# New queue places for the last reads and the tile plan, and new order offsets, in a convolution, Mamba and expert kernel

## Chip, cores and metric

The kernel runs on one core of one Trainium2 chip. Times are device microseconds of one execution. A profile is one further execution, recorded by the hardware profiler; its span runs from the first to the last instruction.

## The reference

The input is two images of 256 channels and 48 by 48 pixels (4608 tokens in all). Layer 0 is a hybrid of local attention and convolution. Layer 1 is a Mamba block over the tokens, followed by a mixture of eight experts of which each token uses two. What matters here is layer 1:

```python
t = t + _L1_attn_ref(_ln_t(t), ...)      # Mamba: projection, convolution, scan over the state, output projection
t = t + _L1_ffn_ref(_ln_t(t), ...)       # experts
# in _L1_ffn_ref:
top_w, top_i = jax.lax.top_k(gate_logits, TOP_K)
for e in range(E):
    h = jax.nn.gelu(xf @ W1[e] + b1[e], approximate=False)
    out = out + w_dense[:, e:e + 1] * (h @ W2[e] + b2[e])
```

## The kernel before

Tokens are worked in 36 chunks of 128 tokens; three chunks make a block of 384. After layer 0 come four parts.

**Mamba.** For each chunk the kernel projects (`cv` for the convolved half, `z` for the gates), turns (`tx`), forms the weighted input `xw`, adds to the state (`pst`), reads it (`ps`, `yi`), multiplies within the chunk (`py`), gates the result (`yz`), sums its squares (`sq`, `sm`, `ss`) and projects it back (`out`). TensorE (PE) does `cv`, `z`, `tx`, `pst`, `ps`, `py`, `ss` and `out`; GpSimd (POOL) does `dx`, `xw`, `yb`, `yz`, `sm` and `rg`; the others do the rest. `keep` stores the finished chunk to the table `acc` in DRAM.

**Gates and stores of rows.** The chunks are gated in seven groups, `GROUPS = (6, 6, 6, 6, 6, 4, 2)`. A group computes logits, the two best experts, and a row for each token and expert in the table `xs` (`place`, `row`, `g10`). `u2` writes the normalised token, and `put` (L1678) stores it with an indirect DMA that POOL issues, two for each chunk, 72 in all.

**Early tiles.** One expert, the one with most rows among the first 24 chunks, begins before Mamba ends: three tiles of 256 rows are fetched from `xs` (`efetch`, on SP, the queue of SyncE; there is room for one in SBUF at a time), turned on PE (`et`), copied by ScalarE (`ext`), and run through `eu` (L1804, up), `eg` (L1812, gelu), `ed` (L1820, down). `ea` (L1832, on VectorE) adds the bias, `es` (L1839) scales by `eweight` (L1788), which is reduced from `eown` (L1780, on POOL), and `eput` (L1842) adds the rows to `acc` with an accumulating indirect DMA. There are two places for the outputs of `ea`, so the third tile's waits for the first tile's two `eput`.

**Usual tiles.** `plan` computes on VectorE which expert and which rows every further tile has. SP loads these values, fetches rows (L2024) and weights (L2014, L2016), and 37 tiles follow: `turn`, `up` (L2080), `down` (L2123 or L2108), `finish` (L2089 scale, L2090 accumulating store). The first `turn` is queued on VectorE behind the last early `ea`.

**Results.** The sums in `acc` are read back in twelve blocks (`load_sums`, L2195), turned on PE (L2219), copied by VectorE and ScalarE (L2222) and stored (L2225) by SP and by ScalarE's queue in turn. Blocks 0 to 7 are read while the last usual tiles run. Blocks 8 to 11, the late reads, wait for the last accumulating store.

The order of Mamba, of the gates and of the early tiles is written by a planner, `Flow`. Every operation has an engine, a cost in nanoseconds, needs and buffers; the planner runs through a model of time, and of the operations that are ready on an engine the one with the lowest rank goes first. The rank is the due time of its chunk less the longest tail of work behind it less an offset for its kind:

```python
return {k: o["due"] - tail[k] - self.lead.get(self.kind(k), 0) for k, o in self.ops.items()}, after
```

The offsets are the table `LEAD1`. What the planner traces is the order in which the engines and SP work; only POOL's order is bound more loosely, by `issue_after` (issue order alone). All of `experts` and `results` is outside the planner: a scheduler orders it within its dependencies, with `issue_after` and `keep_in_program_order` where the code says so.

Of the kernel before, what the change touches and what calls it, by code (L numbers as in the profile page):

```python
# [37 lines left out]
P = 128  # L38
# [32 lines left out]
E, HID = 8, 1024  # L71
NHC = HID // P

TR = 256
CAP = B * N
PART = CAP + TR
EARLY, NEARLY = 3, 3
# [151 lines left out]
class Kernel:  # L229
# [688 lines left out]
    def mamba(self, ctx):  # L918

        nc = self.nc
        self.ps = self.pool("ps", 1, space=bass.MemoryType.PSUM)
        self.used_banks = ["zbank0", "zbank1"]

        room = dict(bank=6, zbank=2, cvbank=2, t=3, xn=2, xc=2, bc=3, cz=2, z=2, btt=2, xd=3, xw=2,
                    mt=4, yi=1, y=4, sq=2, state=3, rd=2, u2=2, ex=1, ext=1, ehid=2, ey=2)
        self.begin_flow(self.pool("m", 1, ctx), room, self.PACE1, self.LEAD1)
        zeros = self.pool("cz", 1, ctx)
        self.cz = [zeros.tile([P, 2, TB], F32, name=f"cz{i}") for i in range(room["cz"])]  # L930
        for t in self.cz:
            nc.gpsimd.memset(t, 0.0)
        for k in range(B * NBLK):
            self.norms(k)
            self.project_block(k)
            self.decays_of(k)
            for c in range(k * NJ, (k + 1) * NJ):
                self.chunk(c)
        first = 0
        for g, n in enumerate(GROUPS):  # L940
            self.gate(g, first, n)
            first += n
        self.early_expert(sum(GROUPS[: EARLY + 1]))
        for i in range(NEARLY):
            self.early_tile(i, sum(GROUPS[: EARLY + 1]))
        self.run_flow()

    PACE1 = 16387
    LEAD1 = {
        "al": -287523, "begin": 279332, "btt": 547186, "ct": -286059, "cum": -1917, "cv": 4243,  # L950
        "decayed": 580164, "dg": 31429, "dt": 47275, "dx": -122176, "ea": -540346, "ebegin": 83800,
        "ed": -318255, "efetch": 54828, "eg": -25970, "eown": -201872, "eplan": -259253,
        "eput": -235403, "er": 11828, "es": -860893, "et": -422487, "etoken": -124013,
        "eu": -436657, "ew": 409693, "eweight": -208246, "ex": -43880, "ext": 233628, "from": -4920,
        "g10": -236552, "g5": 182590, "g6": -32896, "g8": 451102, "g9": -229727, "ge": 6967,
        "gm": 76638, "gmrs": 125702, "grs": 147058, "gsm": -98577, "gsw": -443388, "gw": -513534,
        "head": -233622, "kap": 45673, "keep": -259171, "lg": 101202, "mm": 234795, "mo": -242501,
        "mrs": 274104, "msw": -365601, "mt": -42112, "n2": -300607, "nt": 130491, "number": -184813,
        "out": -70294, "pg": -24498, "place": -128574, "ps": 331262, "pst": 114708, "put": -219828,
        "py": 171510, "rd": 184258, "rg": -26951, "row": 47214, "rs": 219345, "rs1": -133005,  # L960
        "s0": 349893, "s4": 378544, "s5": 226237, "scores": -354133, "silu": -107647,
        "silub": 149134, "silux": 61236, "sm": 498786, "spread": -381240, "sq": -108133,
        "sr": -62966, "ss": -24463, "st": -62401, "state": -200685, "stats": -473991, "su": -4356,
        "tap": 199461, "tb": 11998, "tc": 509331, "tx": 705626, "u2": -301346, "xc": 387790,
        "xd": 75748, "xo": 176627, "xt": 78392, "xw": 264171, "ya": 88604, "yb": 4326, "yi": -10587,
        "yz": -93682, "z": -15541,
    }

    def norms(self, k):
# [556 lines left out]
    def gate(self, g, first, n):  # L1526
# [3 lines left out]
        nc, T = self.nc, self.tiles  # L1530
# [118 lines left out]
        def place():  # L1649
# [5 lines left out]
           uses=[("bank", ("count", g))])  # L1655
# [19 lines left out]
        for i, c in enumerate(chunks):  # L1675
            for q in range(2):
                def put(i=i, c=c, q=q):
                    ins = nc.gpsimd.indirect_dma_start(  # L1678
                        self.xs, bass.IndirectOffsetOnAxis(ap=of("rows")[:, i, q : q + 1], axis=0), T["u2", g][:, i, :],
                        None,  # L1680
                    )
                    self.tc.declare_no_dep(ins.ins, group="rows", reason="every row of the table is written once")
                    self.tc.add_to_no_dep_group("rows", ins.ins)
                    if c >= sum(GROUPS[: EARLY + 1]):
                        self.tc.add_to_no_dep_group("late rows", ins.ins)

                op(("put", (c, q)), "POOL", 1020, put, ("g10", g), ("g8", g), ("u2", c), ("number", g), uses=[("u2", g)])


    def flat(self, b):  # L1690
# [55 lines left out]
    def early_tile(self, i, seen):  # L1746
# [82 lines left out]
        def add():  # L1829
            at = 3 + self.flow.slot["ey", i]  # L1830
            y = T["ey", i] = self.x[1][:, :, at * TR : (at + 1) * TR]
            self.last_add = vec.tensor_tensor(y, T["bank", ("ed", i)].rearrange("p (j q) -> p j q", j=2),  # L1832
                              bcast(bt[:, NHC : NHC + C], 1, [P, 2, C]), ALU.add)

        op("ea", "DVE", 690, add, ("ed", (i, NHC // 2 - 1)), *free, takes=[("ey", i)], uses=[("bank", ("ed", i))])
        for j in range(2):
            def scale(j=j):
                y = T["ey", i][:, j, :]
                nc.scalar.activation(y, y, AF.Identity, scale=T["eweight", i][:, j : j + 1])  # L1839

            def put(j=j):
                ins = pool.indirect_dma_start(  # L1842
                    self.acc, bass.IndirectOffsetOnAxis(ap=T["etoken", i][:, j : j + 1], axis=0), T["ey", i][:, j, :],
                    None, compute_op=ALU.add,
                ).ins
                self.tc.declare_no_dep(ins, group="early", reason="a token has one row of an expert")
                self.tc.declare_no_dep(ins, group="late keeps", reason="later chunks have other rows")
                self.tc.add_to_no_dep_group("early", ins)

            op(("es", (i, j)), "ACT", 390, scale, ("ea", i), ("eweight", i))  # L1850
            op(("eput", (i, j)), "POOL", 1500, put, ("es", (i, j)), ("etoken", i), *[("keep", c) for c in range(seen)],
               uses=[("ey", i)])

    def plan(self):

        nc, begun = self.nc, [5 * TR] * NH
        n, k, tid = P, CAP // TR, self.c["tid"]
        tri = self.c["tri"].rearrange("p (a b) -> p a b", a=E)

        def new(*shape, dtype=F32):  # L1860
            size = int(np.prod(shape))
# [15 lines left out]

        last_rows = new(E, dtype=I32)
        vec.tensor_scalar(last_rows, self.taken, 1.0, None, ALU.add)
        rows = new(3, E)  # L1880
        vec.tensor_sub(rows[:, 0, :], self.taken, self.begin)
        vec.tensor_scalar(rows[:, 1, :], rows[:, 0, :], float(-P), None, ALU.add)
# [60 lines left out]
        for which, row, behind in ((pwhich, prow, late), (swhich, srow, None)):  # L1943
# [14 lines left out]
            vec.tensor_scalar(to[:, 0, :], row, float(E * PART), None, ALU.min)  # L1958
            vec.tensor_scalar(to[:, 1, :], which, float(E - 1), float(P), ALU.min, ALU.mult)
            where.append(to)  # L1960
        return last_rows, where, many

    def value(self, ap, engines, most):

# [12 lines left out]
    def experts(self, ctx):  # L1977
# [159 lines left out]
                    finish(i, y, j)  # L2137
            del weights[i], turned[i], hidden[i]

        ends, where, many = self.plan()  # L2140
        for e in range(E):
            fill(e)
        load(0)
# [2 lines left out]
        load(1)  # L2146
        load(2)
        fetch(2)
        with self.tc.issue_after(self.last_add.ins):
            turn(0)  # L2150
            weight_sums(0)

# [38 lines left out]

    def load_sums(self, g, group=None):

        nc = self.nc
        get = (nc.sync, nc.scalar)[g % 2 if group is None else 0].dma_start(  # L2195
            self.sums_block(g), self.acc[g * TB : (g + 1) * TB, :].rearrange("(p j) c -> p j c", j=NJ)
        )
        if group:
            self.tc.add_to_no_dep_group(group, get.ins)

    def results(self, pool):

        nc = self.nc

        first, size, n = BEFORE // NJ, 2 * TB, 0
        for g in range(0, B * NBLK, 2):
            b, blk = divmod(g, NBLK)
            if g == first:
                for i in range(first, B * NBLK):
                    self.load_sums(i)  # L2210
            for k in range(NH):
                if n % (WMAT // size) == 0:
                    space = pool.tile([P, WMAT], F32, tag="wt", name="o")
                o = space[:, n % (WMAT // size) * size :][:, :size].rearrange("p (i t) -> p i t", i=2)
                n += 1
                for i in range(2):
                    ps = self.bank()
                    for j in range(NJ):
                        nc.tensor.transpose(  # L2219
                            ps[:, j * P : (j + 1) * P], self.sums_block(g + i)[:, j, k * P : (k + 1) * P], self.ident  # L2220
                        )
                    (nc.vector.tensor_copy, nc.scalar.copy)[i](  # L2222
                        o[:, i].rearrange("c (p j) -> c j p", j=NJ), ps[:, :TB].rearrange("c (j p) -> c j p", j=NJ)
                    )
                (nc.sync, nc.scalar)[k].dma_start(self.out[b, k * P : (k + 1) * P, blk * TB : (blk + 2) * TB], o)  # L2225
# [133 lines left out]
```

## Time and profile before

| what | value |
|---|---|
| median of 3 runs | 1307.5 us |
| the runs | 1303.49, 1307.5, 1307.64 us |
| the profiled execution | 1306.41 us, span 1304.4 us |
| PE, share of the span busy | 95% |
| PE weight load | 75% |
| VectorE (DVE) | 71% |
| ScalarE (ACT) | 61% |
| POOL | 43% |
| indirect stores L1678 | 72, 72.7 us busy on POOL |

Shares are averages over stages with different limits. A line of who waited for whom gives engine, tile and line, then what ended the wait, then the total in us, how many times, and the longest. A line of the timeline gives start and length in us, engine, line, operation, tiles and shapes, and in brackets the idle time of the engine before it with what ended it. A row of busy time by stretch gives the stretch, its length, the busy us of PE, PE's weight load, DVE, ACT and POOL, then the granted PE clock, the busy share of the DMA engines, and GB/s. PE's matmuls overlap each other, so that their ends are modelled.

### The profile page before, as it was taken

The page shows a single profiled execution, that of the slowest core. Times are in us where ns is not written, and L with a number is a line of the kernel's source. Part 1 is how long each engine was busy: PE and PEld are TensorE (multiplying, and loading weights), DVE is VectorE, ACT ScalarE, POOL GpSimd, SP SyncE. Part 2 cuts the span into 40 slices and gives each one's busy share as a digit, 9 for nine tenths or more (in the row PEclk, how much of TensorE's full clock was granted, in tenths as well). Part 3 has the DMA queues.
Part 4 walks back from the last instruction along what each step waited for, and adds up shares of the span by engine and source line. Part 5 has one row for each costly group of instructions (what it writes and reads, how often), then busy time and mean ns, then how long its engine had stood idle before and what let it go on. Part 6 is the DMA issues. An engine that isn't in the chain of part 4 may idle for free.

```text
span 1304.4 us, 23542 instructions
## 1 busy us (share of the span) xinstructions
PE 1237.6 (95%) x8048; PEld 984.3 (75%) x8048; DVE 929.0 (71%) x2425; ACT 796.3 (61%) x1956; POOL 557.9 (43%) x769
## 2 busy tenths in 40 slices
PE   4999999997899999999999998999999999999995
PEld 3566766665567776767676787999999999999994
DVE  5899999999577878888787654655655565556442
ACT  2598968898899877979696742433343333333342
POOL 4312230210367798879888872222221212221220
PEclk9999999999799999999999998999999999999998
DMA  8331322211132243424446148567667657766756
GB/s 297 109 103 41 117 83 79 74 50 31 65 99 80 85 133 101 139 89 160 137 122 189 54 142 277 156 191 247 184 228 227 212 183 234 234 190 199 231 176 206
DMA packets 101657, 194.10 MB, mean 149 GB/s; under 512 B 10635, under 2 KB 82652, under 8 KB 96604
## 3 DMA queue, kind: packets, MB, share of 16 engines
q1 hardware_dynamic: 84732, 167.72, 38.2%
q0 software_dynamic: 14400, 19.74, 7.9%
q10 hardware_dynamic: 2404, 5.11, 1.1%
q8 instruction: 65, 1.06, 0.3%
q14 instruction: 56, 0.46, 0.1%
HBM read 154.24 MB, written 43.23 MB: 151 GB/s over the span
## 4 chain that ended last, share of the span: by engine, by line
PE 46%; POOL 10%; DVE 3%; issue 3%; ACT 2%; DMA 1%; ACTq 0%; SPq 0%; DVEq 0%; POOLq 0%
PE bank L2080 19%; PE po L2123 15%; POOL xs L1678 4%; PE bank L916 2%; PE bank L1450 1%; PE po L2108 1%; PE bank L902 1%; PE zbank L916 1%; POOL sq L1457 1%; POOL y L1424 1%; POOL y L1442 1%; PE bank L1820 1%; PE bank L1432 1%; PE bank L1804 1%; POOL y L1331 1%
## 5 line engine op out<-in xcount | busy, mean ns | idle before, releaser
L2090 POOL DMA_INDIRECT acc<-ey,token x70 | 109.2, 1560 | 368.0 <-ACT ey L2089 322.9
L2080 PE MATMUL bank<-ext,wt 128*128 128x256 f32 (+1 forms) x1152 | 241.3, 368 | 0.0
L2084 ACT ACTIVATE hid<-bank,bt 128x256 f32<-128x256 f32 (+1 forms) x288 | 132.4, 461 | 170.9 <-PE bank L2080 166.6
L2080 PEld LDWEIGHTS bank<-ext,wt 128*128 128x128 f32 x1152 | 207.0, 190 | 25.0
L681 POOL COPY kp<-kp 128x10 f32<-128x10 f32 (+1 forms) x60 | 24.7, 412 | 179.8 <-DVE kp L674 179.8
L592 DVE SCALAR_TENSOR_TENSOR x<-hid,w2r,x 128x1128 f32<-128x1128 f32 (+3 forms) x72 | 100.1, 1394 | 0.4 <-ACT hid L586 0.2
L2123 PE MATMUL po<-ts,ss 128*128 128x128 f32 x768 | 96.2, 275 | 0.0
L916 PE MATMUL bank<-xn,win 128*128 128x387 f32 x240 | 93.0, 511 | 1.6 <-ACT t L998 1.6
L1128 DVE SCALAR_TENSOR_TENSOR xc<-bank,vec,xc 128x384 f32<-128x384 f32 x144 | 86.7, 612 | 9.2 <-ACT xc L1117 8.6
L2123 PEld LDWEIGHTS po<-ts,ss 128*128 128x128 f32 x768 | 90.9, 192 | 0.0
L1344 ACT ACTIVATE mt<-mt,cum 128x128 f32<-128x128 f32 x288 | 87.9, 394 | 0.0
L800 ACT ACTIVATE prob<-prob,top 128x308 f32<-128x308 f32 x144 | 78.4, 553 | 15.3 <-DVE top L789 15.0
L1678 POOL DMA_INDIRECT xs<-u,rows x72 | 72.7, 1009 | 16.0 <-issue 14.3
L2127 ACT COPY u<-po 128x128 f32<-128x128 f32 x32 | 8.5, 266 | 113.9 <-PE po L2123 113.9
L1450 PE MATMUL bank<-wout,y 128*128 128x264 f32 x288 | 71.3, 392 | 1.2 <-DVE yi L1409 1.2
L2067 DVE TENSOR_TENSOR ss<-hid 128x512 f32<-128x512 f32 x32 | 22.1, 691 | 70.3 <-ACT hid L2084 70.3
L916 PE MATMUL zbank<-xn,win 128*128 128x384 f32 x192 | 71.0, 491 | 0.3 <-ACT z L1246 0.3
L806 ACT ACTIVATE prob<-prob,rden 128x308 f32<-128x308 f32 x144 | 67.8, 552 | 3.7 <-DVE rden L855 3.7
L582 DVE SCALAR_TENSOR_TENSOR hid<-xp,vec,hid 128x1175 f32<-128x1175 f32 (+1 forms) x48 | 68.5, 1428 | 0.1
L2123 PE MATMUL po<-wt,hid 128*128 128x128 f32 x496 | 65.5, 275 | 0.0
L789 DVE CUSTOM_DVE_ANT_0 prob<-banks,cst 128x308 f32<-128x308 f32 x144 | 61.7, 473 | 4.9 <-PE banks L779 4.6
L916 PEld LDWEIGHTS bank<-xn,win 128*128 128x128 f32 x240 | 43.2, 196 | 23.9 <-issue 3.7
(335 smaller groups left out, 3004.2 us busy)
## 6 DMA issues: line engine op xcount, KB each, us to landing
wt<-in_We SPq DMA_DIRECT2D x36, 2048.0 KB
mt<-decays SPq DMA_DIRECT2D x36, 512.0 KB
ex<-xs SPq DMA_DIRECT2D x36, 265.0 KB
rd<-decays SPq DMA_DIRECT2D x68, 128.0 KB
val<-vtab SPq DMA_DIRECT2D x72, 110.0 KB
bt<-in_We SPq DMA_DIRECT2D x36, 136.0 KB
vraster<-vout SPq DMA_DIRECT2D x18, 256.0 KB
acc<-x SPq DMA_DIRECT2D x36, 128.0 KB
```

Of the source, the lines that this page charges most:

```text
L582: nc.vector.scalar_tensor_tensor(dst, src, w[:, k : k + 1], dst, ALU.mult, ALU.add)
L592: nc.vector.scalar_tensor_tensor(dst, src, w[:, k : k + 1], dst, ALU.mult, ALU.add)
L800: nc.scalar.activation(t, t, AF.Exp, bias=T["top", c][:, a : a + 1], scale=-1.0, accum_out=T["den", c][:, a : a + 1])
L916: self.nc.tensor.matmul(ps, lhsT=lhs(k), rhs=rhs(k), start=k == 0, stop=k == NH - 1)
L1128: nc.vector.scalar_tensor_tensor(out(), T["bank", ("cv", at)][:, i : i + TB], wc[:, i : i + 1], out(), ALU.mult, ALU.add)
L1344: nc.scalar.activation(t, t, AF.Relu, bias=at_s, scale=-1.0)
L1450: nc.tensor.matmul(ps[:, : C + E], lhsT=T["y", c][:, m, :], rhs=self.l1["wout"][:, m, :], start=m == 0, stop=m == NZ - 1,)
L1678: ins = nc.gpsimd.indirect_dma_start(self.xs, bass.IndirectOffsetOnAxis(ap=of("rows")[:, i, q : q + 1], axis=0), T["u2", g][:, i, :], None,)
L2080: nc.tensor.matmul(ps[:, :rows], lhsT=w1[:, k, c * P : (c + 1) * P], rhs=xt[:, k, :], start=k == 0, stop=k == NH - 1,)
L2084: nc.scalar.activation(hid[:, c, :], ps[:, :rows], AF.Gelu, bias=bt[:, c : c + 1])
L2090: put = nc.gpsimd.indirect_dma_start(self.acc, bass.IndirectOffsetOnAxis(ap=token[:, j : j + 1], axis=0), y, None, compute_op=ALU.add)
L2123: nc.tensor.matmul(p[name], lhsT=v[a][:, c], rhs=v[w][:, c], start=c == 0, stop=c == NHC // 2 - 1)
```

## The change

It has four parts.

1. All late reads go to SP, one after another in program order, which is behind the four early stores of SP in `results`. Before, two of the four were on ScalarE's queue, and both pairs stood ahead of the stores.
2. `plan` is split: the first part computes the ends of the experts' rows, and `plan_tiles` the rest. `plan_tiles` is queued on VectorE behind the second early tile's `ea`. The adds are kept in a table, `self.adds`, in place of `self.last_add`.
3. The planner counts 1315 ns for a `put` in place of 1020, and 1980 for an `eput` in place of 1500.
4. The table `LEAD1` has a new offset for each of its 95 kinds.

```diff
+        self.adds = {}
         self.early_expert(sum(GROUPS[: EARLY + 1]))
...
     LEAD1 = {
-        "al": -287523, "begin": 279332, "btt": 547186, "ct": -286059, "cum": -1917, "cv": 4243,
...
+        "al": -290978, "begin": 28518, "btt": 903929, "ct": -258969, "cum": 138318, "cv": 4160,
...
-                op(("put", (c, q)), "POOL", 1020, put, ("g10", g), ("g8", g), ("u2", c), ("number", g), uses=[("u2", g)])
+                op(("put", (c, q)), "POOL", 1315, put, ("g10", g), ("g8", g), ("u2", c), ("number", g), uses=[("u2", g)])
...
-            self.last_add = vec.tensor_tensor(y, T["bank", ("ed", i)].rearrange("p (j q) -> p j q", j=2),
+            self.adds[i] = vec.tensor_tensor(y, T["bank", ("ed", i)].rearrange("p (j q) -> p j q", j=2),
...
-            op(("eput", (i, j)), "POOL", 1500, put, ("es", (i, j)), ("etoken", i), *[("keep", c) for c in range(seen)],
+            op(("eput", (i, j)), "POOL", 1980, put, ("es", (i, j)), ("etoken", i), *[("keep", c) for c in range(seen)],
...
         last_rows = new(E, dtype=I32)
         vec.tensor_scalar(last_rows, self.taken, 1.0, None, ALU.add)
+        return last_rows, partial(self.plan_tiles, new, piece)
+
+    def plan_tiles(self, new, piece):
...
-        ends, where, many = self.plan()
+        ends, plan_tiles = self.plan()
+        with self.tc.issue_after(self.adds[NEARLY - 2].ins):
+            where, many = plan_tiles()
...
-        with self.tc.issue_after(self.last_add.ins):
+        with self.tc.issue_after(self.adds[NEARLY - 1].ins):
             turn(0)
             weight_sums(0)
...
-        get = (nc.sync, nc.scalar)[g % 2 if group is None else 0].dma_start(
+        get = self.nc.sync.dma_start(
...
-                    self.load_sums(i)
+                    self.tc.keep_in_program_order(self.load_sums(i))
```

## Prediction

> **What bounds the kernel now.** I read the slices of the page first, then the busy time by stretch, then who waited for whom in Mamba, in the early tiles and at the end. The slices show four stages: layer 0 to about 322 us, Mamba to about 752 (the last output projection), the rest of the early tiles to 800, 37 usual expert tiles to 1280, and the results.
>
> ```profile
> PE   4999999997899999999999998999999999999995
> ...
> POOL 4312230210367798879888872222221212221220
> ...
> 350.00:745.00 395.00, 381.47 (x2419) 274.73 (x2418) 320.49 (x908) 325.83 (x765) 325.17 (x440) 0.99 0.40 119
> 815.00:1247.00 432.00, 432.00 (x2922) 404.22 (x2921) 250.53 (x644) 155.30 (x365) 99.88 (x64) 1.00 0.67 210
> ```
>
> The columns after the length are busy PE, weight load, DVE, ACT, POOL. In the expert stage PE never stops (432.00 of 432.00), and nothing the change touches is in it: no gain there. In Mamba PE works 381 of 395 us, and POOL 325, to which the pauses around its 72 indirect stores come. Waits, PE in 440 to 745, then POOL in 440 to 783:
>
> ```profile
> PE bank L1460 <- POOL sq L1457: 6.0, 6, 2.1
> PE bank L1370 <- POOL xw L1316: 2.5, 2, 2.1
> PE bank L1432 <- DVE mt L1352: 1.2, 2, 1.0
> ...
> POOL xs L1678 <- issue: 14.3, 65, 0.3
> ```
>
> So what PE loses in Mamba it loses mostly to POOL (8.5 us), and POOL's stores (L1678) cost 0.3 us each beyond their own 0.99: a store follows a store after 1.28 us (770.48, 771.76, 773.13 in the timeline), where the plan counted 1020 ns. The early tiles:
>
> ```profile
> DVE eweight L1788 <- POOL eown L1780: 8.9, 1, 8.9
> ...
> PE bank L1820 <- ACT x L1812: 5.2, 1, 5.2
> ...
> 782.18 0.17 DVE L1788 TENSOR_REDUCE eweight<-eown 128x2 f32<-128x16 f32 x1 [8.93 <-POOL eown L1780]
> ...
> 786.75 0.68 DVE L1832 TENSOR_TENSOR x<-bank,wt 128x512 f32<-128x512 f32 x1
> ...
> 788.79 3.06 PEld L1820 LDWEIGHTS bank<-wt,x 128*128 128x128 f32 x8 [5.59 <-ACT x L1812]
> 788.79 3.78 PE L1820 MATMUL bank<-wt,x 128*128 128x256 f32 x8 [5.18 <-ACT x L1812]
> ```
>
> Read upwards: PE stands for 5.2 us, for a gelu on ACT; ACT stood at the scale behind the add L1832; the add stood on DVE behind the plan (782.3 to 786.7) and this behind eweight, which waited 8.9 us for eown on POOL, queued behind the last stores. After the stall eight matmuls take 3.78 us instead of 1.89. The first usual tile starts at 800.23. The end:
>
> ```profile
> ACT o L2222 <- DMA acc<-ey,token: 4.9, 1, 4.9
> ...
> 1282.00:1284.00 2.00, 0.02 (x1) 0.00 (x0) 0.72 (x2) 0.00 (x0) 0.00 (x0) 1.00 0.59 66
> ...
> 1292.00:1294.00 2.00, 1.99 (x16) 1.54 (x16) 0.86 (x2) 1.21 (x2) 0.00 (x0) 1.00 1.03 416
> ```
>
> ACT holds two of the four late reads, which wait for the last scatter (landed at 1283.7), and its copies for the early output stand behind them for 4.9 us; from 1286 to 1302 the DMA engines are full (381 GB/s mean).
>
> [...]clock 0.54 from 788.8 to 795.2 behind the 5.2 us stall. [...]1283 ns a load; the trace has 1.28 us. The order has 33 loads instead of 35, but ACT is not at its limit, so I count nothing.
>
> **The change part by part.** The sum is made against the profiled execution, 1306.4 us (span 1304.4). [...]
>
> *New offsets and costs of the stores.* No instruction is added; the five engines' orders change in Mamba. I read both orders and made running totals of measured durations: POOL from its groups (yz 1.274, yb 1.276, dx 1.044, xw 1.040, a pair of sq sums 1.19, rg 0.564, a store 1.28), PE from the chain (out 1.78 a chunk, py 1.02, ps 1.09, a cv or z block 1.3, an up or down step 1.75, the rest from its groups). Totals hardly differ: POOL's last store ends after 395.5 us of work before and 395.9 after; PE has 445.3 in both. What differs is how they mesh. POOL runs behind PE by a lag. For POOL not to wait, the lag must be at least PE's total ahead of py (or tx) less POOL's ahead of yz (xw) of that chunk; for PE not to wait, at most PE's total ahead of out, ss or pst less POOL's ahead of yz, sq or xw. From chunk 8 on, the room between the highest lag asked so far and the lowest allowed after is, in the order before, 1.7 us at chunk 12 (37.3 less 35.6), 1.9 at 18, 1.6 at 25, 2.0 at 30; in the new order 3.5 at 14, 4.5 at 24, 4.2 at 31, 3.3 at 35. A hand-over takes POOL's 1.27 and DVE's 0.69, 2.0 us together: the old order has less than that in four places, the new one nowhere. Of the 8.5 us that PE waited for POOL I take 5 as gone; between a gain of 10 and a loss of 4, since DVE and ACT are not in these totals.
>
> *Early tiles, by the same offsets.* POOL's eown for the third tile stands ahead of 16 stores (before: behind all). So eweight no longer stops DVE, and the chain of 5.2 us goes, with its slow clock (3.78 and 2.82 us for steps of 1.89: 2.8 us): 8 us. What is late next: eown waits for SP's fetch of that tile, this for its transpose, which PE does at 413.8 in its total; with 0.6 for PE, 0.6 for ACT's copy and 3.2 for the fetch (763.99 to 767.14 before) that is 418.2, and from eown to the end of the last store POOL's total has 21.1: about 440 on PE's scale, 5 us ahead of PE's own end (445.3 and some 2 for gates and table loads). The third add then waits for the first pair of early scatters: issued at 440.3 and 442.2, landing 3.7 to 9.8 us later by the rows of L2090, mostly 5.3: 447.5; add 0.69 and the copy L904 0.69: 449. Before, the zero of that scale, its waits so far included, stood at 343.3 by the last two chunks (out at 748.6, total 405.3), and the first tile started 456.9 behind it (800.2). 8 us is thus the best; with 4 us of later landing and a cold start I take 4, from 0 to 8.
>
> *Plan of the tiles behind the add of the second early tile.* Some 60 DVE instructions (at most 11.2 us: 766.6 to 773.2 and 782.3 to 786.9) move as a block between the second and third add. PE has 14 us of the third tile's work there (8 steps of 1.75): this covers them, the third add standing behind. Behind the plan SP's fetch of tile 1 and its weights are queued; they issue near 445 on that scale, and 2.2 MB at 400 GB/s (what 800 to 812 show) need 5.5 us[...]: 453, against 463 when tile 1 begins. 0. In exchange the 2.1 us for which DVE stood in front of `place` (763.98 to 766.10, at the plan's memset) go; those are in the stores' chain, counted above.
>
> *Late reads.* Two reads move from ACT to SP, and all four stand behind SP's four early stores; ACT is free of the 4.9 us. Sixteen copies of 0.6 to 0.69 us on two engines: early output goes out from about 1282 to 1287 instead of 1285 to 1291, the DMA engines fill some 2.5 us sooner. Against it: the reads issue at 1287 to 1289 instead of 1284 to 1285, four issues of 0.43 us on one queue, [...]landed near 1295.5 (before about 1292), then transposes, copies, two stores, with the engines partly idle for 1 us. Sixteen transfers of 0.39 MB, 6.3 MB, at 410 GB/s from 1283.5 give 1299[...]: gain 1.5, from 3 to a loss of 1.
>
> Sum: 5 + 4 + 1.5 = 10.5 of 1306.4, so 1295.9; the median stands 1.1 higher: **1297**.
>
> **The rivals.** (a) POOL was not the limit of Mamba: DVE or ACT (321 and 326 of 395) take its waits over, nothing from Mamba: 1302. For: both as busy as POOL; against: PE waits for them under 3 us. Chance 0.20. (b) The landing of early scatters holds the first tile: L1842 shows 10.6 to 12.0 us to landing where weights are loading. Then the third add comes at 453, PE idles over 5 us and restarts cold (3 us): nothing from the early tiles, 1301. Against: the first pair starts before the weights. Chance 0.18. (c) Slower: POOL stops at the early eown, with all 16 stores behind it. ACT's copy for its fetch stands behind u2 copies that wait for stores to land, and two table loads; each us it is late moves the last store, the scatters and the first tile. It decides beyond 8 us; at 14, with Mamba unchanged: 1306.4 + 6 - 1.5, so 1312 by the median. Chance 0.09. The change does do what it says: the orders show it.
>
> **How the numbers follow.** Forecast 0.53, own range 1290 to 1303. About 0.3%, 3.9 us, is what can be told from no change here. All of the forecast, 0.13 of (a) and 0.11 of (b) are faster: 0.77; the rest of those two, same: 0.14; (c) 0.09. The range, 1289 to 1306, leaves out (c) and a tenth.
>
> **What would show it.** Right: PE's wait for sq and xw under 3 us; no L1820 stall; no eweight wait of 8.9; the first usual tile (now L2085) before 796, and 480 us from it to the last scatter as before; ACT's copies of the results without a DMA wait. Wrong: Mamba's last out not earlier; POOL waiting at eown; DVE's third add waiting for DMA; reads landing so late that the DMA engines empty.

## The result and the profile after

Four runs of the changed kernel have a median of 1295.0 us (1292.3 to 1296.5), against 1307.6 beside them: a ratio of 0.991 (0.988 to 0.994). A second set gave 1292.3 against 1306.3, 0.9894 (0.9879 to 0.9909). So it is faster by about 1%, and the forecast of 1297 us has the right size. The time did not come from the stages in the shares that the forecast gave them.

I begin with the slices of the first profile after (span 1294.0 us), and its busy time in two stretches. Both stretches are moved 10 us earlier than those of before, since everything came that much earlier; the columns are as before.

```profile
PE   4999999998799999999999997999999999999995
...
POOL 4411230210357878999889963212121212221220
```

```profile
340.00:735.00 395.00, 388.36 (x2468) 280.01 (x2468) 323.44 (x925) 334.83 (x788) 326.38 (x445) 1.00 0.39 119
805.00:1237.00 432.00, 432.00 (x2920) 404.15 (x2919) 250.62 (x649) 155.25 (x365) 99.36 (x64) 1.00 0.67 213
```

The page looks the same at a glance: the same valley near 320 us and one where the early tiles end. The gain is in the first stretch, where PE is busy for 388 of 395 us in place of 381. The expert stage is untouched. The PE waits from 440 to 745 us, all that are listed:

```profile
PE bank L1390 <- DMA cz<-bc: 2.2, 2, 1.5
PE bank L1433 <- DVE mt L1353: 0.6, 1, 0.6
PE bank L1220 <- issue: 0.3, 1, 0.3
```

No line names POOL any more: the 8.5 us for `sq` and `xw` are gone. The second profile of the changed kernel names POOL in none of PE's Mamba waits either. A table by stage shows what each part gave. "Again" is the second profile of the changed kernel, the other rows are experiments that follow; `out` is that of the last two chunks, and all times are us from the span's start.

| kernel | last `out` starts | first usual tile | (after `out`) | results start | (after first tile) | end | (results) |
|---|---|---|---|---|---|---|---|
| before | 748.6 | 800.2 | 51.6 | 1280.1 | 479.9 | 1304.4 | 24.3 |
| changed, first | 738.2 | 790.7 | 52.5 | 1270.6 | 479.9 | 1294.0 | 23.4 |
| changed, again | 737.1 | 785.4 | 48.3 | 1267.1 | 481.7 | 1290.0 | 22.9 |
| order only | 740.1 | 787.1 | 47.1 | 1268.7 | 481.6 | 1293.7 | 25.0 |
| plan only | 748.5 | 794.7 | 46.1 | 1276.2 | 481.6 | 1301.0 | 24.8 |
| reads only | 748.2 | 799.7 | 51.5 | 1279.4 | 479.6 | 1304.4 | 25.0 |
| offsets only | 756.5 | 806.1 | 49.6 | 1286.0 | 479.9 | 1310.8 | 24.8 |
| costs only | 748.1 | 801.7 | 53.7 | 1281.6 | 479.9 | 1306.5 | 24.9 |
| reads in the middle | 736.0 | 787.0 | 51.0 | 1266.9 | 479.9 | 1290.2 | 23.3 |

In the row "costs only" the `out` is that of the last chunk alone, since its planner had put the other one ahead; that makes its Mamba look about 1.8 us later than it is.

Mamba gave 10 to 11 us, the early tiles nothing in the first profile, the results about 1. In the results ScalarE's copies wait for no DMA any more, but PE does, in the first profile after:

```profile
PE bank L2226 <- DMA x<-acc: 7.4, 1, 7.4
```

In the early tiles the 5.2 us stall and the 8.9 us wait for `eown` are gone, but in the first profile PE stands again. Two engines of its timeline:

```profile
770.92 0.84 ACT L1813 ACTIVATE x<-bank,wt 128x256 f32<-128x256 f32 x2 [1.63 <-PE bank L1805]
771.64 1.89 PE L1805 MATMUL bank<-x,wt 128*128 128x256 f32 x8
...
783.09 1.75 ACT L1813 ACTIVATE x<-bank,wt 128x256 f32<-128x256 f32 x4 [11.34 <-remote]
783.62 5.70 PE L1821 MATMUL bank<-wt,x 128*128 128x256 f32 x16 [6.64 <-issue]
...
790.70 7.17 PE L2085 MATMUL bank<-ext,x 128*128 128x256 f32 x32 [0.94 <-DVE ext L904]
```

ScalarE's third gelu of the last tile needs the matmuls that end at 773.5, yet starts at 783.1; "remote" says that the trace knows no releaser. PE waits 6.6 us for it and runs 16 matmuls in 5.70 us where 3.62 is usual. The second profile does not have this hold (below), so I tested first whether it belongs to the change.

### The profile page after: what moved, and what is told of

It is laid out like the page before. It is cut to its first block, busy times and chain, and to the rows that moved or that the text cites. A ratio compares the mean times of both kernels' runs of the same rounds, so it can differ in the third digit from the quotient of the medians.

```text
span 1294.0 us, 23558 instructions
## 1 busy us (share of the span) xinstructions
PE 1232.5 (95%) x8048; PEld 983.4 (76%) x8048; DVE 924.8 (71%) x2425; ACT 792.7 (61%) x1954; POOL 557.6 (43%) x769
## 5 line engine op out<-in xcount | busy, mean ns | idle before, releaser
L681 POOL COPY kp<-kp 128x10 f32<-128x10 f32 (+1 forms) x60 | 24.9, 415 | 179.4 <-DVE kp L674 179.4
L916 PEld LDWEIGHTS bank<-xn,win 128*128 128x128 f32 x240 | 42.5, 195 | 24.8 <-issue 3.9
```

The source lines that it names most:

```text
L916: self.nc.tensor.matmul(ps, lhsT=lhs(k), rhs=rhs(k), start=k == 0, stop=k == NH - 1)
```

## The experiments

**The changed kernel again, and each part alone** (one chip, before at 1306.3). The edits are the parts of the diff: "reads only" has part 1, "plan only" part 2, "order only" parts 3 and 4.

> The changed kernel once more. In its first profile ScalarE's third gelu of the last early tile (L1813) starts 11.3 us after the one before, with no releaser that the trace knows, PE stands for 6.6 us and runs cold for 16 matmuls after it, and VectorE's plan takes 9.4 us where the same second half took 4.4 us before. Theory: something that belongs to this order holds them, so it comes back: again 4 to 11 us of PE standing between 770 and 785, the first usual tile at 789 to 792, 1295 in the median. Rival: it was an accident of that one execution: then PE stands for less than 2 us there, the first usual tile starts near 783 to 786, and this profile's span is 1286 to 1289.

0.9894 (0.9879 to 0.9909), span 1290.0. The timeline of PE from 775 on, with VectorE's third add:

```profile
775.77 3.62 PE L1821 MATMUL bank<-wt,x 128*128 128x256 f32 x16
...
782.32 1.09 PE L902 MATMUL bank<-cst,ex 128*128 128x128 f32 x4 [2.93 <-issue]
...
784.08 0.69 DVE L1833 TENSOR_TENSOR x<-bank,wt 128x512 f32<-128x512 f32 x1 [6.45 <-DMA acc<-x,etoken]
...
785.42 8.93 PE L2085 MATMUL bank<-ext,x 128*128 128x256 f32 x32 [2.01 <-DVE ext L904]
```

The hold did not come back here, as the rival said, but the span fell by 4 us only, to 1290 (the rival had 1286 to 1289): now PE ends the third tile at 779.4 and stands until the turn of the first usual tile (L902), whose fetch goes at 778.5, behind POOL's last store (775.3). Then it waits for VectorE, whose copy L904 stands behind the third add; the add waits 6.5 us for the first tile's scatters to land. Hence two pauses of 2.9 and 2.0 us and a cold start: 8.93 us for 32 matmuls in place of 7.17, at a granted clock of 0.60 from 785 to 790.

> The kernel before with the new offsets and the new costs alone; late reads and plan as before. Theory: nearly all of the change is Mamba: the last two chunks' out starts near 738 in place of 748.6, the early tiles give nothing more, the results 24.3 us: 1298 to 1297, 9 to 10 us less. Here most of the plan stands ahead of the second add on VectorE; if that costs, PE stands 2 to 5 us more at L1820 and it is 1300 to 1302. Rival: the gain needs the split plan or the reads: 1303 or more.

0.9892 (0.9874 to 0.9909), median 1292.15, 14 us less than before where 9 to 10 were expected: within these intervals the whole gain of the change. The plan ahead of the second add costs PE only 1.4 us (773.38 in its timeline). Its third add waits 12.9 us for the landing of the first scatters, and PE, after one pause of 2.6 us, begins the first usual tile cold (8.86 us for 32 matmuls in place of 7.17).

> The kernel before with the plan of the tiles alone behind the second early add. On VectorE the add then comes right behind eweight instead of 4.4 us later; on the other engines no instruction moves. Theory: the 5.2 us for which PE stood at L1820 shrinks to under 1.5 us and its 2.8 us of slow clock goes, but the third add then waits for the landing of the first early scatters, so the first usual tile gains 3 to 6 us: 1302 to 1305. Rival (the prediction's zero for this part, taken over to the old order): what the second add gains the third loses behind the plan, within 1 us of before.

0.9983 (0.9975 to 0.9992), median 1303.5. The 5.2 us stall is gone as expected, and the first usual tile gains 5.5 us, less 1.7 for a cold start (8.86 us for 32 matmuls in place of 7.17). Two of its waits:

```profile
DVE eweight L1789 <- POOL eown L1781: 15.2, 1, 15.2
...
PE bank L2085 <- DVE ext L904: 3.5, 1, 3.5
```

VectorE now stands 15.2 us in place of 8.9, because the plan no longer fills part of that time; the whole plan follows the second add, and the third add with L904 behind it is late by 3.5 us.

> The kernel before with the late reads alone as in the change (all four on SP, behind its four early stores); Mamba, the early and the usual tiles as before. Theory: from the first matmul of the results to the end of the span 23.4 us in place of 24.3, as in the changed kernel, so 0.9 us less: 1306.5 if before stands at 1307.5. Rival, the size of the prediction or more: 1.5 to 3 us less, because ScalarE's 4.9 us wait goes: 1304.5 to 1306. Rival on the other side: reads that land late cost more than the wait: 1308 or more.

0.9988 (0.9980 to 0.9997), median 1304.7: 0.4 to 2.6 us. Its profile shows no gain in the results (25.0 us): ScalarE's wait is gone, but PE waits 7.5 us for the reads. So each of the parts outside the order, put alone into the kernel before, gives 2.8 and 1.6 us by the medians; beside the new order they give nothing that these runs can tell.

**Is it POOL?** (On a second chip, where before took 1309.8 and has no profile.) `sm` returns without emitting its adds, before and changed:

```diff
         def sm(n):
             sq = T["sq", c]
-            nc.gpsimd.tensor_add(sq[:, :n, :], sq[:, :n, :], sq[:, n : 2 * n, :])
+            return
```

The square sums change the routing of tokens, so only the times up to the last `out` are read, not the totals (1336.8 and 1340.0 us, with other tiles).

> The kernel before, leaving out POOL's two adds a chunk that fold the squares (L1457, 36 x 1.19 = 42.8 us of POOL); the square sums are so taken over a quarter of the columns. No instruction of another engine moves. Theory: PE lost its time in Mamba to a POOL that came late, so with a lighter POOL the old order loses it no more: the last two chunks' out starts 7 to 10 us earlier than the 748.2 to 748.6 of the old order, at 738 to 741, PE's waits for sq and xw are under 1 us, and the whole is 1296 to 1299. Rival (the prediction's a): VectorE and ScalarE take the waits over: out at 745 or later, 1302 or more.

The last `out` starts at 738.8. PE's wait for `sq` on POOL is gone, the one for `xw` is down from 2.5:

```profile
PE bank L1370 <- POOL xw L1316: 1.0, 1, 1.0
```

PE's idle time from the first projection to the last `out` is 5.7 us in all, in place of 13.5. A lighter POOL in the old order gives 9.9 us, as much as the new order: that a late POOL cost Mamba its 10 us is shown, since the orders of PE, VectorE and ScalarE did not move. That the new order gains through POOL too rests on its waits for POOL being 0; no run moves POOL's order alone.

> The same left out of the changed kernel. Theory: in the new order PE does not wait for POOL any more, so there is nothing left to win in Mamba: out within 2 us of the 737 to 738 of the changed kernel. Rival: the new order only hides a part, and POOL is still the limit: out at 734 or earlier.

At 742.4, 4 to 5 us later than the changed kernel; neither theory. PE waits for POOL nowhere by name, but 2.7 us at 478.3 before `out`, whose input `yz` came at 476.1 in place of 472.6. POOL's stores are bound loosely, and three more of them had slipped ahead of it. So here stores ahead of a gate product cost PE directly, and more than the pause: `out` behind it takes 3.71 us in place of 1.95. That POOL has nothing left to give in the new order is not shown cleanly.

**Offsets or costs?** On the same chip, before at 1309.8.

> The kernel before with the new offsets alone, stores still counted at 1020 and 1500 ns. Theory: offsets and costs belong together; the planner that takes the stores for shorter than they are puts POOL's work in another order, and half the gain or more is lost: out at 742 to 746, 1297 to 1303. Rival: the offsets do it alone: out at 737 to 740, 1292 to 1295.

1.0051 (1.0034 to 1.0068), slower than before, and last `out` at 756.5 in its profile, which is its fastest execution (1312.6 of a median of 1316.0). PE's longest wait is that for `sq` again, 11.2 us in place of the 6.0 of before:

```profile
PE bank L1460 <- POOL sq L1457: 11.2, 7, 4.9
```

> The kernel before with the new costs alone (1315 and 1980 ns), old offsets. Theory: costs closer to the truth do not help without offsets that fit them: out at 746 to 752, 1304 to 1311. Rival: the true pitch of the stores is what matters: out at 743 or earlier, 1301 or less.

1.0055 (1.0038 to 1.0072). Its profile too is its fastest execution (1308.4 of a median of 1316.3), so it does not show all of the loss; the wait for `sq` is 9.6 us there. Both theories were too kind: parts 3 and 4 each lose alone and together give the whole gain. So the new offsets do not carry over to the old costs, nor the old offsets to the new costs. (Both profiles also have the hold told of under "Open", 4.9 and 6.3 us at the longest, so a part of the 0.5% may be the chip's; the late `out` of the offsets is not.)

**Three repairs** of the changed kernel, on a third chip, before at 1309.6, and the three together (`all3`). Each stands with its diff.

```diff
-        ), ("u2", first))
+        ), ("u2", first), ("put", (first - 1, 1)) if g == len(GROUPS) - 1 else None)
```

> The changed kernel with one need more: the last group's number (L1663, POOL) comes behind the last store of the group before it. In the changed kernel it stands ahead of six such stores and stops POOL for 2.4 us at 761 to 763.5, until ScalarE has a free u2. Theory: the early tiles now end with POOL's stores: the last one 2.4 us earlier (773 in place of 775.3), so the fetch of the first usual tile and the early scatters too, the first usual tile at 783 in place of 785.4[...]: ratio to before 0.986 to 0.988 where the changed kernel has 0.9894. Rival: the first usual tile hangs on something else (its weights, the plan): within 0.5 us of 785.4 less what Mamba differs, ratio unchanged.

0.9902 (0.9887 to 0.9916), no gain. POOL's pause is gone (stores at 761.56, 762.82, 764.09, 765.35, 766.62), but the planner filled the place with two early scatters at 767.9 and 769.9, and the last store stayed at 775.6. The first usual tile came at 792.8, behind waits of the unexplained kind (ScalarE 6.7 us, VectorE 15.0).

```diff
-                    mt=4, yi=1, y=4, sq=2, state=3, rd=2, u2=2, ex=1, ext=1, ehid=2, ey=2)
+                    mt=4, yi=1, y=4, sq=2, state=3, rd=2, u2=2, ex=1, ext=1, ehid=2, ey=3)
...
-            y = T["ey", i] = self.x[1][:, :, at * TR : (at + 1) * TR]
+            if self.flow.slot["ey", i] == 2:
+                y = T["ey", i] = self.large_tile("ey", i, [P, 2, C])
+            else:
+                y = T["ey", i] = self.x[1][:, :, at * TR : (at + 1) * TR]
```

> The changed kernel with a third place for the outputs of the early tiles, so that the third add does not wait for the landing of the first tile's scatters (6.4 us in the second profile of the changed kernel). Theory: the wait goes, but the fetch of the first usual tile, behind the last store, is next: its turn on PE stays at 782.3, the copy L904 follows at once in place of 784.7, the first usual tile at 784.1: 1.3 us gained, ratio 0.988. Rival: the landing is the bound, 3 us or more gained: 0.987 or less.

0.9983 (0.9974 to 0.9993): by the ratios about 12 us worse than the changed kernel. SP and PE show why (this profile has the hold told of under "Open" too, 11.3 us on ScalarE, which makes its scatters later still):

```profile
SPq L2032 <- DMA acc<-ey,etoken: 18.7, 1, 18.7
...
PE bank L902 <- DVE token L2050: 10.9, 1, 10.9
```

SP's fetch for the first usual tile waits 18.7 us, until the third tile's scatters have landed (issued at 790.2 and 792.1; the fetch goes at 796.4). The third place came from Mamba's pool, whose memory the usual tiles take over: that the fetched rows lie in it is my reading of this wait. The edit moved the wait from an add to a fetch.

```diff
-            if g == first:
+            if g == first - 4:
...
-                (nc.sync, nc.scalar)[k].dma_start(self.out[b, k * P : (k + 1) * P, blk * TB : (blk + 2) * TB], o)
+                put = (nc.sync, nc.scalar)[k].dma_start(self.out[b, k * P : (k + 1) * P, blk * TB : (blk + 2) * TB], o)
+                if k == 0:
+                    self.tc.keep_in_program_order(put)
```

> The changed kernel with the four late reads behind two of SP's early stores in place of four. Theory: the reads issue at about 1271 to 1274.5 on the clock of the second profile instead of 1274.4 to 1278.4, their data come 2 to 3 us earlier than 1280.9, and the 2 us in which the DMA engines are half empty (0.41 at 1282 to 1284) go: the results take 21 to 21.8 us in place of 22.9, ratio 0.988. Rival: SP stops at the reads until the last scatter has landed and its two other early stores come so much later that nothing is gained: 22.9 or more.

0.9863 (0.9845 to 0.9882), 1292.35 against 1309.6: the best ratio measured. The reads' first data release PE 10.1 us after the start of the results (1277.0) in place of 13.8 (1280.9), and the DMA engines no longer empty (their busy share is 0.97 or more in every row of 2 us from 1270 to 1286). Nearly all of this is the time at which SP comes to the first read: 4.1 us after that start (1270.9) in place of 7.3 (1274.4). The stretch of 2 us in the second profile of the changed kernel, then in this one (the last two columns are DMA share and GB/s):

```profile
1282.00:1284.00 2.00, 2.00 (x11) 2.00 (x10) 1.12 (x2) 1.00 (x2) 0.00 (x0) 0.51 0.41 164
```

```profile
1282.00:1284.00 2.00, 1.49 (x7) 1.14 (x6) 0.80 (x2) 1.06 (x2) 0.00 (x0) 0.67 1.05 420
...
1288.00:1290.20 2.20, 0.00 (x0) 0.00 (x0) 0.00 (x0) 0.00 (x0) 0.00 (x0) 0.50 0.02 7
```

But the results take 23.3 us in this profile, not 21 to 21.8, which is the rival's mark: the transfers end sooner and the last 2 us pass with the DMA engines idle. Why they do is not shown; in the profile of `all3`, which has the same edit, the results take 21.7 us. The interval touches that of the changed kernel, measured on another chip. So it has the best ratio of the study, and is not shown to beat the changed kernel.

> The three edits together. Theory: the gains lie on one path one after the other and add up, except that the third place is worth little once the stores come earlier: first usual tile at 781 to 782.5, results 21 to 21.8 us, 1285 to 1288 if before stands at 1306.5, ratio 0.983 to 0.986. Rival: with the stores earlier PE's own end of the third tile (779.4) and the turn behind it hold the start at 783 or later: ratio 0.986 to 0.988.

1.0016 (1.0006 to 1.0025): the third place's cost is in it (PE waits 11.1 us at L902), and the first usual tile comes at 805.8.

## Why the prediction was right, and where it was not

**Mamba: 5 forecast, 10 to 11 measured** (last `out` at 748.6, then at 737.1 and 738.2, less 0.6 for the four transposes of an early tile, which no longer stand ahead of it). The mechanism held: PE's waits for POOL are 0 (forecast under 3), and `before_no_sums` shows that POOL was the cause. That the new order frees PE by the wider room between the lags, from which the prediction argued, was not tested by itself. Mis-sized was the term "of 8.5 us I take 5 as gone". From the first projection to the last `out`, 416.1 us became 403.4 in the second profile. Listed waits fell from 13.2 to 6.3: all 8.5 for POOL, with 1.6 more for DMA and VectorE. The other 5.6 us is PE's own busy time, 402.5 to 396.9, for nearly the same matmuls (the four transposes take 0.6 of it).

Most of the rest is the granted clock. By rows of 2 us, before has two stretches in this part of Mamba in which the clock is down to half (0.78, 0.50 and 0.86 from 558 to 564; 0.51 and 0.64 from 740 to 744), each right behind one of its two longest waits for POOL (2.06 and 2.12 us). What these rows lack of the full clock is 1.7 us in each stretch. The second profile after has none. The first of them, and the same place in `reads only`, whose Mamba has the old order too:

```profile
558.50 0.65 PE L1370 MATMUL bank<-xw,btt 128*64 128x256 f32 x4 [2.06 <-POOL xw L1316]
...
560.32 1.45 PE L1219 MATMUL bank<-cst,a 128*8 128x128 f32 x6
```

```profile
558.24 0.65 PE L1370 MATMUL bank<-xw,btt 128*64 128x256 f32 x4 [2.05 <-POOL xw L1316]
...
559.52 0.82 PE L1219 MATMUL bank<-cst,a 128*8 128x128 f32 x6
```

So a wait for POOL cost more than its idle time, which is all that the term counted. But it did not do so each time: in `reads only` the same wait has full clock behind it, and that profile has one slow stretch and 400.7 us of busy PE. The first profile after also has one (640.8 to 644.4), with no wait ahead of it, and 398.2 us. What decides is not shown, and of the 5.6 us some 1.6 stay unexplained.

**Early tiles: 4 forecast, 1.5 measured at best.** In the second profile 51.6 us became 48.3, and 1.8 of these 3.3 went into the cold start that the first profile lacks. The step "of 8 us at most I take 4" was too large for what it named as due next: the first early scatters, and a cold restart. The landing itself was as forecast (in the second profile 5.6 us from the issue of the second scatter, 778.5, to the third add, where 5.3 was taken), but POOL came to it later: from `eown` to the end of its last store 24.1 us pass (752.1 to 776.2) where the running total has 21.1, and 2.6 of that is POOL's pause for `u2` ahead of `number`. So what rival (b) described came in part (the third add held by scatters, PE standing and restarting cold), though not for its reason, a landing of 10.6 us or more: in `order only` too it is 5.6. The mark "first usual tile before 796" was met thanks to Mamba, and one of the prediction's signs of being wrong showed: the third add waits for DMA (6.4 us here, 12.9 in `order only`).

**The plan: 0 forecast**, and in the new order none shown: order only and the changed kernel have 0.9892 and 0.9894. It is worth 2.8 us only in the old order, where the stall it removes exists. (The working takes 400 GB/s from 800 to 812; that row shows 381, which makes 0.3 us and changes nothing. What it allows beyond the transfer was the author's estimate.)

**Results: 1.5 forecast, 0.9 and 1.4 in the two profiles.** ScalarE's 4.9 us wait went, as forecast. On the other side the reads came late, as it also said: PE waits 7.4 and 7.6 us for `x<-acc` and restarts cold (granted clock 0.50 from 1284 to 1288 in the first profile, 0.50 and 0.51 from 1280 to 1284 in the second), and the DMA engines empty in part, a second sign of being wrong. That gap was put at 1 us; by rows of 2 us (0.41 and 0.83 from 1282 to 1286 in the second profile) it comes to some 1.5. Between its 1299 and its gain of 1.5 the working has 2.9 us beyond that gap, the author's estimate; in before 2.4 us pass at the end behind the last row with busy DMA engines (share 0.94 from 1301 to 1302, 0.09 to 1303, 0.00 to 1304.4). The landing of the reads near 1295.5 was an estimate too, and that stores ahead of them on SP hold their data back is not shown: from the issue of the first read to PE's release 6.4 us pass with four of SP's stores ahead and 6.1 with two (`reads_mid`), so nearly all of the 3.6 us that `reads_mid` gains there is the earlier issue.

So the sum, -10.5, met the first profile's -10.4 of span with a Mamba term half as large as what was measured and two others too large: that the errors cancel is luck. Rival (a) is refuted by `before_no_sums`; rival (c) did not happen (the fetch for the third early tile went at 748.2, and POOL did not wait at `eown`).

**Open:** the hold with no releaser. It is in the first profile of the changed kernel and in all eight profiles of the second and third chip of the experiments (the longest in each 4.9 to 15.0 us, both orders), and in none of the four of the first chip, nor in that of before. In the first of these VectorE's plan steps from 774 to 783 come mostly 0.71 us apart, and its trace has fewer records of semaphore events: 2073 of VectorE, where the second profile of the same kernel has 2157. So it is with all nine: 2066 to 2101, where the five others have 2151 to 2157. The fewer records may be why no releaser is named; why an engine is late they do not say. What causes the hold, and whether executions without a profile have it, no run here shows.

## What to carry to other kernels

When an engine in the middle (here POOL) serves a full one, ask by how much its queue may lag before the full engine stops, and test it by making that engine lighter without moving anything else. A planner's costs and its priorities were one setting here: each changed alone lost 0.5%, together they gained 1.1%. When you price a wait of a full engine, look at the clock behind it as well as at its idle time (here 1.7 us more behind each of two waits of 2.1 us). Behind a removed wait, work out what is due next at the same join (here the landing of scatters, the fetch, VectorE's queue) before booking the gain, and look whose memory a new buffer takes.

## What was unexpected of the hardware

- In before, waits of PE of 2.06 and 2.12 us were each followed by a stretch at half clock, worth 1.7 us more (granted clock 0.78, 0.50 and 0.86 from 558 to 564; 0.51 and 0.64 from 740 to 744). In `reads only` the same wait of 2.05 us was not followed by it.
- One pause of 2.62 us in `order only`, and two of 2.93 and 2.01 us with 1.09 us of matmuls between them in the second profile after, gave cold starts of 1.7 and 1.8 us (8.86 and 8.93 us for 32 matmuls in place of 7.17).
- Before took 1306.3 us on one chip and 1309.6 and 1309.8 on two others, the ones whose profiles show the hold.
